# Moving the counts, near_f and the epoch boundaries of a graph layer's planner

## The chip, the cores and the metric

One core of one Trainium2 chip runs the whole program in one launch. The time is the device time of that core in microseconds.

## The reference

For a graph of 6250 nodes and 206250 edges (each random edge in both directions, and a loop at each node) the layer computes a message per edge, a mean over each node's edges, a node network, and a residual layer norm:

```python
msg = jnp.concatenate([x[col], edge_attr], axis=1)       # 64 + 64
h = jax.nn.relu(msg @ W1a.T + b1a) @ W1b.T + b1b         # 128, then 64
sums = segment_sum(h, row, n_nodes)
agg = sums / jnp.maximum(counts, 1.0)[:, None]
z = jax.nn.relu(jnp.concatenate([x, agg], 1) @ W2a.T + b2a) @ W2b.T + b2b
out = jnp.concatenate([z, x], axis=1) @ Wr.T + br
return layernorm(x + out)
```

`row` is the source of an edge, `col` its destination. All is float32. Edges come sorted by destination, so the sources are in no order: the sum over sources is a sort.

## The kernel before

The edges are padded to 1612 tiles of 128 and taken in 124 blocks of 13 tiles (`NG`, `BLK`), in a fixed order that spreads the destinations. The 6250 nodes lie in 49 bins of 128. The fast path sorts edges by bin through memory. A slower general path stands behind it, for inputs that overflow the planner's bounds, which are worked out from means and 4.8 deviations (`SPREAD`).

**A block k** goes through these steps. `group` (three blocks ahead) loads the edge features and the destinations' places; `columns` turns the places into one-hot columns of a window of 64 nodes. `window` computes the first layer's share of those nodes and puts it into the weights `mv`. For the first 8 blocks (`NEAR`) it does this from x itself, and `columns` compares the destinations with `near_f` on VectorE (DVE, L1184). `hidden` (L1206) multiplies 13 tiles of columns by `mv` on TensorE (PE), in portions of 4, 3, 3 and 3 tiles, and ScalarE (ACT, L1209) writes the ReLU into one of five row buffers `orows`. A first write into a buffer (L1507) waits until the scatters of block k-5 have landed.

`carried` and `bins_of` (both two blocks ahead of their use) make one-hots of the edges' bins and scan them along the free axis on DVE (`had`, L936). `counts_of` (L972 to L975, for block k+1) turns them into ranks by PE in a PSUM tile named `cnt`. `slots` reduces those on DVE to an edge's row in memory (`rowidx`, L1000); `quads` does it for joined edges (reading `cnt` up to `at_q`, L1059). `scatter` (called for block k-2) issues one indirect DMA per tile from GpSimd (POOL, L1245). Here the manual order of PE, ACT, DVE, and SyncE (SP) doesn't hold: the framework's scheduler places the scatters, and each block's last ones are held until PE has reached stated points of block k+2.

**Joined groups.** Blocks from `JOIN_FROM` to `JOIN_TO` join the first three tiles (six, in blocks 8 to 61) before they are scattered: `join` (L1115) puts edges of the same bin into rows of four by PE, and one scatter (L1217) writes a joined group into `quads`.

**Sums.** The blocks are parted into four epochs (`EPOCHS`), each with a buffer in memory of its own. A bin has a fixed number of row tiles in each (`cap`), which is what its edges can at most fill; up to `low` tiles are surely filled. When an epoch's scatters, or a stretch of the first epoch's, are done, SP reads its tiles back from four blocks later on (`LATE`), DVE makes one-hots of the nodes (`oh`, L1333), and PE sums (L1352, two PE instructions for a tile). The groups of a stretch are spread evenly over the blocks until the next stretch ends; `groups_at` holds this. `clear` writes zeros ahead of time into the tiles between `low` and `cap`.

**The end.** `nodes_ahead` (L1474 to L1484) computes what the node network needs of x alone, four bins a block from block `PRE`. After the last block the groups of the last epoch are read, summed, and each group is finished and written (`Nodes`).

The iteration for block k (from L1500) has this order on each engine; the start, ahead of it, is: `window(0)`, `carried(0)`, `counts_of(0)`, `columns(0)`, `slots(0)`.

Of the kernel before, what the change touches and what calls it, by code (L numbers as in the profile page):

```python
# [8 lines left out]
F32 = mybir.dt.float32  # L9
# [8 lines left out]
P = 128  # L18
# [430 lines left out]
NG = 13  # L449
WIN = 64  # L450
STEP = 43
EPOCHS = (104, 12, 4, 4)
NEAR = 8
Y_AHEAD = 32
HEAD = 117
# [4 lines left out]
RD = 6  # L460
SUMS, TILES = 3, 12
SEG = 9
PRE = 102
RING = 8
ROWS, EDGES, READS = 5, 4, 9
SPREAD = 4.8
# [1 line left out]
CLEAR = 12  # L468
LEAD = 2
JOIN, QUAD, QROWS = 3, 4, 3  # L470
JOIN_FROM, JOIN_TO = 5, 104
TWICE_FROM, TWICE_TO, TWICE_ROWS = 8, 62, 5
FULLQ = (7, 9)

# [1 line left out]
def order_of(ngr):  # L476


    return [i * STEP % ngr for i in range(ngr)]
# [3 lines left out]
def fast_path(  # L483
# [41 lines left out]
    REM = N - (NB - 1) * P  # L525
    NE = len(EPOCHS)
    W = H + 2
# [4 lines left out]
    order = order_of(NGR)  # L532
    assert NT % NG == 0 and NGR == sum(EPOCHS) and HEAD % BLK == 0 and sorted(order) == list(range(NGR))

# [10 lines left out]
    def joined(k):  # L545
        if not JOIN_FROM <= k < JOIN_TO:
            return 0
        return 2 if TWICE_FROM <= k < TWICE_TO else 1

    def direct(k):  # L550
        return BLK - JOIN * joined(k)
# [39 lines left out]
    epochs, at_blk = [], 0  # L591
    for e, n in enumerate(EPOCHS):
        ep_ = Epoch()
# [25 lines left out]
    qep.first, qep.end = JOIN_FROM, JOIN_TO  # L619
    assert JOIN_TO == EPOCHS[0]  # L620

# [28 lines left out]
    const = ctx.enter_context(tc.tile_pool(name="fconst", bufs=1))  # L650
# [91 lines left out]
    with (  # L742
# [80 lines left out]
        def starts_at(joints):  # L823


            if joints:
                d = BLK - JOIN * joints
                nc.vector.memset(words, 1.0 + 0x3F80 * 2.0**-23)
                v = words.rearrange("p (b t) -> p b t", t=TJ)
                for c in (0, d + 1, TJ, TJ + d + 1):  # L830
                    if c % 2 == 0:
                        nc.vector.memset(v[:, :, c // 2], 1.0)
                    else:
                        nc.vector.memset(v.bitcast(I32)[:, :, c // 2], 0x3F80)
            else:
                v = words[:, : HALF * T]
                nc.vector.memset(v, 1.0 + 0x3F80 * 2.0**-23)
                nc.vector.memset(v.rearrange("p (b t) -> p b t", t=T // 2)[:, :, 0], 1.0)
# [9 lines left out]
        bins(0, HEAD)  # L848

        cnt = slpp.tile([P, 2, 512], F32, name="cnt_ps")  # L850
        near_f = cnt[:, 1, 448 : 448 + NEAR]
        z_ps = steady[:, P + 2 + HALF * TJ :][:, : 2 * JOIN]
        of_first = cnt[:, :, HALF * TJ : HALF * TJ + HALF]
        assert T % 2 == 0 and TJ % 2 == 1
# [60 lines left out]
        def bins_of(k):  # L915


            ep_ = epoch_of[k]
            c0 = k * BLK
            oh = ohs.pop(k)  # L920
            if joined(k) != joined(k - 1):
                starts_at(joined(k))
            t = TJ if joined(k) else T
            had = slp.tile([P, 2 * HALF * t], BF16, name="had", padded_shape=[P, 2 * HALF * TJ])
            by_bin = oh.rearrange("p (b t) -> p b t", t=t)
            d = direct(k)
            for t0, c, n in ((1, c0 + BLK - d, d), (d + 2, c0, BLK - d)):
                if n == 0:
                    continue
                nc.vector.tensor_tensor(  # L930
                    by_bin[:, :, t0 : t0 + n],
                    ramp[:, : 2 * HALF, None].to_broadcast([P, 2 * HALF, n]),
                    hi[:, None, c : c + n].to_broadcast([P, 2 * HALF, n]),
                    op=ALU.is_equal,
                )
            nc.vector.tensor_tensor_scan(had, on[:, : 2 * HALF * t], oh, 0.0, op0=ALU.mult, op1=ALU.add)  # L936
            oh, had = (v.rearrange("p (b t) -> p b t", t=t) for v in (oh, had))
            hads[k] = had
            return oh, had
# [23 lines left out]
        def counts_of(k, oh, had):  # L963
            t = oh.shape[2]

            ps = cnt
            for i in range(2):
                v = ps[:, i, : HALF * t].rearrange("p (b t) -> p b t", t=t)  # L970
                b = slice(i * HALF, (i + 1) * HALF)
                nc.tensor.matmul(v, one_w, had[:, b, :], start=True, stop=False)  # L972
                nc.tensor.matmul(v[:, :, : t - 1], before_w, oh[:, b, 1:], start=False, stop=True)  # L973
                if joined(k) == 2:
                    nc.tensor.matmul(of_first[:, i, :], one_w, had[:, b, direct(k) + 1 + JOIN], start=True, stop=True)  # L975
            return ps
# [171 lines left out]
        def group(g):  # L1148

            rhs = rhss[g % EDGES]  # L1150
            if g < NEAR:
                all_of = dst[g * NG * P : (g + 1) * NG * P].rearrange("(o e) -> o e", o=1)
                s = nc.sync.dma_start(rhs[D:, :].bitcast(I32), all_of.to_broadcast([WIN, NG * P]))
                edges(g)
                with tc.issue_after(s.ins):
                    w = nc.sync.value_load(win_i[0:1, g : g + 1], min_val=0, max_val=N - WIN)
                nc.sync.dma_start(near[:D, g, :], xT[:, bass.ds(w, WIN)])
                return rhs, None, mv[g % MV]
            edges(g)

            half = NG * P // 2
            rel = rhs[D:, :].bitcast(BF16).rearrange("p (h e) -> p h e", h=2)[:, :, half:]
            s = nc.sync.dma_start(
                rel, relt[g : g + 1, :].rearrange("o (h e) -> o h e", h=2).to_broadcast([WIN, 2, half])
            )
            with tc.issue_after(s.ins):
                w = nc.sync.value_load(win_i[0:1, g : g + 1], min_val=0, max_val=N - WIN)
            m = mv[g % MV]
            nc.sync.dma_start(m[D:, :], ytab[bass.ds(w, WIN), :])
            return rhs, rel, m  # L1170

        def columns(g, part_of=0):


            rhs, rel, _ = made[g]
            if g >= NEAR:
                of_win = rhs[D:, :].rearrange("p (h e) -> p h e", h=2)
                if part_of == 0:
                    nc.scalar.activation(of_win, rel, AF.Square, bias=from_win[D:, :])  # L1179
                else:  # L1180
                    nc.scalar.activation(rhs[D:, :], rhs[D:, :], AF.Relu, bias=ones[D:, :1], scale=-1.0)  # L1181
                return
            if part_of == 0:
                nc.vector.tensor_tensor(  # L1184
                    rhs[D:, :], rhs[D:, :].bitcast(I32), near_f[D:, g : g + 1].to_broadcast([WIN, NG * P]),
                    op=ALU.is_equal,
                )

        def window(g):

            ps = hp.tile([P, H], F32, name="h_ps")
            nc.tensor.matmul(ps[D:, :], near[: D + 1, g, :], w1x_t, start=True, stop=True)
            nc.scalar.copy(mv[g % MV][D:, :], ps[D:, :])
# [5 lines left out]
        def hidden(k, parts):  # L1199
            orow = orows[k % ROWS]  # L1200
            rhs, _, m = made[k]
            for k0, n in parts:
                ps = hp.tile([P, SUB, H], F32, name="h_ps")
                for j in range(n):
                    c = k0 + j
                    done[k, c] = nc.tensor.matmul(  # L1206
                        ps[:, j, :], rhs[:, c * P : (c + 1) * P], m, start=True, stop=True
                    ).ins.name
                nc.scalar.activation(orow[:, k0 : k0 + n, :H], ps[:, :n, :], AF.Relu)  # L1209
# [244 lines left out]
        clears.update({6 + 2 * i: (-1, i) for i in range(CLEAR)})  # L1454
        assert max(clears) < EPOCHS[0] and 5 + 2 * CLEAR <= EARLY

# [36 lines left out]
        )  # L1493
        for g in range(3):
            made[g] = group(g)
        window(0)
        carried(0)
        counts = counts_of(0, *bins_of(0))
        columns(0)
        slots(0, counts)  # L1500
        for k, ep_ in enumerate(epoch_of):
# [15 lines left out]
            if k == 0:  # L1517
                hidden(k, ((0, 4), (4, 3), (7, 3), (10, 3)))
                window(1)
                columns(1)  # L1520
                carried(1)
                ahead = bins_of(1)
            if k + 1 < NGR:
                counts = counts_of(k + 1, *ahead)
            if k + 2 < NGR:
                carried(k + 2)
            if k > 0:
                hidden(k, ((0, 4), (4, 3), (7, 3)))
            if k + 2 < NEAR:
                window(k + 2)  # L1530
            if k == NEAR - 6:
# [25 lines left out]
            if k == 4:  # L1557
# [19 lines left out]
                centred(wrx_t)  # L1577
            if 0 <= k - PRE < -(-NB // SUB):
                nodes_ahead((k - PRE) * SUB)
            if k in clears:  # L1580
# [206 lines left out]
```

## Time and profile before

| | |
|---|---|
| three timed runs | 1740.62, 1749.65, 1750.46 us; median 1749.65 |
| profiled execution | 1742.9 us, its span 1741.1 us |
| mean granted clock of TensorE | 0.953 |
| busy: PE, DVE, ACT, POOL | 1495.1 (86%), 1451.1 (83%), 900.1 (52%), 1255.2 us (72%) |
| DMA | 408.89 MB, mean 235 GB/s |
| scatters on POOL | 1153 of single tiles, 153 of joined groups |
| sums on PE (L1352) | 4202 instructions |

A busy share is an average over the stages: the start, blocks 8 to 61 with two joined groups, 62 to 103 with one, the last 20 without, and the end. An engine can set the pace of all of them without being busy all the time, where it has a fixed pause between its instructions. In the timeline, each row is the start, the time, the engine and line, and in brackets the idle time ahead of it with what ended it.

### The profile page before, as it was taken

Reading aid. Unit: us, or ns where it says so; the run is one execution under the profiler, and the core shown is the slowest. Engines: PE = TensorE matmul, PEld = TensorE weight load, DVE = VectorE, ACT = ScalarE, POOL = GpSimd, SP = SyncE. Lnnn points to the kernel's source line nnn. Section 1 sums busy time; section 2 is a strip of 40 time slices with the busy share of each in tenths; the row PEclk is TensorE's granted clock in tenths of the full one; section 3 lists DMA queues with packets and bytes.
Section 4 is the critical chain, followed back from the end, with each engine's and each line's share of the span. In section 5 each row is a group of like instructions: output and inputs, shape, how many; then the busy total and the mean of one; then the engine's idle time right before and its main releaser. Section 6 shows DMA issues by size and latency. Waiting matters only on the chain. (4 is left out here: it accounts for less than half of the span.)

```text
span 1741.1 us, 36105 instructions
## 1 busy us (share of the span) xinstructions
PE 1495.1 (86%) x12229; PEld 1426.3 (82%) x12229; DVE 1451.1 (83%) x3408; ACT 900.1 (52%) x1797; POOL 1255.2 (72%) x1323
## 2 busy tenths in 40 slices
PE   5668888888888888776899999989889999999987
PEld 4568878788878787766798999889889898999976
DVE  8489999999999899766788988989877676888777
ACT  2257777666766666554555555545443333443026
POOL 5777777777777777777777777777777777777720
PEclk9789999989999999978999999999999999999998
DMA  8878888856666565558799999879788888999971
GB/s 185 217 242 273 275 271 271 278 175 190 189 189 189 169 200 169 163 167 238 213 267 271 288 286 276 272 233 269 221 248 255 247 239 252 273 322 298 334 231 47
DMA packets 216190, 408.89 MB, mean 235 GB/s; under 512 B 43265, under 2 KB 122740, under 8 KB 215868
## 3 DMA queue, kind: packets, MB, share of 16 engines
q1 hardware_dynamic: 127770, 230.22, 47.1%
q0 software_dynamic: 49136, 117.56, 20.7%
q10 hardware_dynamic: 39090, 58.69, 10.6%
q8 instruction: 100, 1.64, 0.4%
q14 instruction: 94, 0.77, 0.1%
HBM read 228.29 MB, written 178.01 MB: 233 GB/s over the span
## 5 line engine op out<-in xcount | busy, mean ns | idle before, releaser
L1245 POOL DMA_INDIRECT rows<-orow,rowidx x1153 | 1105.8, 959 | 368.6 <-issue 216.0
L1352 PE MATMUL h_ps<-rt,oh 128*128 128x129 f32 x4202 | 511.4, 280 | 44.8 <-DVE oh L1333 17.4
L1352 PEld LDWEIGHTS h_ps<-rt,oh 128*128 128x128 f32 x4202 | 495.1, 196 | 50.6 <-issue 21.6
L1206 PE MATMUL h_ps<-mv,rhs 128*128 128x128 f32 x3224 | 416.2, 285 | 26.3 <-ACT orow L1209 18.4
L1206 PEld LDWEIGHTS h_ps<-mv,rhs 128*128 128x128 f32 x3224 | 397.5, 200 | 38.8 <-ACT orow L1209 21.3
L1209 ACT ACTIVATE orow<-h_ps 128x512 f32<-128x512 f32 x496 | 255.1, 538 | 302.8 <-PE h_ps L1206 296.2
L1333 DVE TENSOR_TENSOR oh<-ramp,rt 128x512 f32<-128x512 f32 (+4 forms) x466 | 332.3, 752 | 26.9 <-DMA rt<-rows 22.3
L1115 PE MATMUL h_ps<-orow,shared 128*128 128x130 f32 (+1 forms) x2376 | 302.6, 285 | 38.9 <-ACT orow L1209 32.6
L1115 PEld LDWEIGHTS h_ps<-orow,shared 128*128 128x128 f32 x2376 | 291.7, 200 | 43.3 <-ACT orow L1209 37.0
L936 DVE TENSOR_TENSOR_SCAN had<-ramp,bins 128x750 bf16<-128x750 bf16 (+1 forms) x124 | 210.6, 1699 | 99.0 <-ACT bins L956 90.3
L1179 ACT ACTIVATE rhs<-rhs,from_win 64x1664 f32<-64x1664 bf16 x116 | 194.6, 1677 | 2.9
L1181 ACT ACTIVATE rhs<-rhs,ones 64x1664 f32<-64x1664 f32 x116 | 194.6, 1677 | 2.9
L1092 DVE TENSOR_TENSOR shared<-quad_ramp,ramp 128x1536 f32<-128x1536 f32 x99 | 173.4, 1751 | 11.0 <-PE h_ps L1115 4.8
L1507 ACT CAST orow<-lo 128x13 f32<-128x13 bf16 x124 | 26.5, 214 | 292.9 <-DMA rows<-orow,rowidx 256.9
L972 PE MATMUL cnt_ps<-had,one_w 128*128 128x375 bf16 (+1 forms) x248 | 81.8, 332 | 85.5 <-DVE at_q L1059 74.0
L1115 PE MATMUL h_ps<-orow,oh 128*128 128x130 f32 (+1 forms) x1296 | 154.3, 275 | 0.0
L1115 PEld LDWEIGHTS h_ps<-orow,oh 128*128 128x128 f32 x1296 | 149.8, 190 | 0.0
L1119 ACT COPY shared<-h_ps 128x260 f32<-128x260 f32 x168 | 62.2, 378 | 109.2 <-PE h_ps L1115 51.1
L930 DVE TENSOR_TENSOR bins<-ramp,hi 128x300 bf16<-128x300 f32 (+2 forms) x223 | 113.7, 548 | 0.3
L1409 DVE TENSOR_TENSOR part<-part,h_ps 128x387 f32<-128x387 f32 (+2 forms) x207 | 89.9, 435 | 21.2 <-PE h_ps L1352 20.4
L973 PEld LDWEIGHTS <-before_w 128*128 128x128 bf16 x248 | 25.5, 103 | 99.9 <-issue 94.3
L1217 POOL DMA_INDIRECT quads<-shared,qidx x84 | 80.6, 960 | 25.6 <-issue 10.7
(161 smaller groups left out, 1291.9 us busy)
## 6 DMA issues: line engine op xcount, KB each, us to landing
rhs<-in_edgeT SPq DMA_DIRECT2D x124, 416.0 KB
rt<-rows SPq DMA_DIRECT2D x106, 390.0 KB
rt<-rows SPq DMA_DIRECT2D x145, 260.0 KB
rt<-quads SPq DMA_DIRECT2D x97, 260.0 KB
rhs<-relt SPq DMA_DIRECT2D x116, 208.0 KB
rows<-padrow ACTq DMA_DIRECT2D x12, 1560.0 KB
rows<-orow,rowidx POOLq DMA_INDIRECT x1153
rt<-rows SPq DMA_DIRECT2D x48, 325.0 KB
```

Source lines behind the costliest of these rows:

```text
L930: nc.vector.tensor_tensor(by_bin[:, :, t0 : t0 + n], ramp[:, : 2 * HALF, None].to_broadcast([P, 2 * HALF, n]), hi[:, None, c : c + n].to_b ...
L936: nc.vector.tensor_tensor_scan(had, on[:, : 2 * HALF * t], oh, 0.0, op0=ALU.mult, op1=ALU.add)
L1092: nc.vector.tensor_tensor(m, quad_ramp.rearrange("p g q -> p (g q)")[:, None, :].to_broadcast([P, JOIN, QUAD * P]), z_ps[:, i * JOIN : (i ...
L1115: done[k, f"join{i}"] = nc.tensor.matmul(ps[:, j, :w], m[:, t, (g0 + j) * P : (g0 + j + 1) * P], orow[:, i * JOIN + t, :w], start=t == 0, ...
L1179: nc.scalar.activation(of_win, rel, AF.Square, bias=from_win[D:, :])
L1181: nc.scalar.activation(rhs[D:, :], rhs[D:, :], AF.Relu, bias=ones[D:, :1], scale=-1.0)
L1206: done[k, c] = nc.tensor.matmul(ps[:, j, :], rhs[:, c * P : (c + 1) * P], m, start=True, stop=True).ins.name
L1209: nc.scalar.activation(orow[:, k0 : k0 + n, :H], ps[:, :n, :], AF.Relu)
L1245: s = nc.gpsimd.indirect_dma_start(out=ep_.rows, out_offset=bass.IndirectOffsetOnAxis(ap=rowidx[:, k % RING * BLK + j : k % RING * BLK + j ...
L1333: nc.vector.tensor_tensor(res[:, at_tile : at_tile + nb * n, :], ramp[:, None, :].to_broadcast([P, nb * n, P]), node[:, :, None].to_broadc ...
L1352: m = nc.tensor.matmul(of_bin(b), oh[:, at_tile, :], rt[:, j * n + t, : H + 1], start=t0 + t == st.lo[b], stop=t0 + t == st.hi[b] - 1,)
L1409: nc.vector.tensor_add(to, to, g.ps[:, : g.nb, :])
```

## The change

Four things are changed:

- The epochs are 106, 10, 4 and 4 blocks long instead of 104, 12, 4 and 4, and blocks 104 and 105 get a joined group (155 groups instead of 153). `nodes_ahead` starts two blocks later (`PRE`).
- Ahead of the first block, `window(0)` stands behind `counts_of(0)` instead of before `carried(0)`.
- In each block but the first, the first portion of `hidden` (four tiles) stands ahead of `counts_of(k + 1)` and `carried(k + 2)`; the second and third stay behind them.
- `near_f` has an SBUF tile of its own. Before, it lay in a corner of the PSUM tile `cnt`.

```diff
-EPOCHS = (104, 12, 4, 4)
+EPOCHS = (106, 10, 4, 4)
...
-PRE = 102
+PRE = 104
...
-JOIN_FROM, JOIN_TO = 5, 104
+JOIN_FROM, JOIN_TO = 5, 106
...
-        near_f = cnt[:, 1, 448 : 448 + NEAR]
+        near_f = const.tile([P, NEAR], F32, name="near_f")
...
-        window(0)
         carried(0)
         counts = counts_of(0, *bins_of(0))
+        window(0)
         columns(0)
...
+            if k > 0:
+                hidden(k, ((0, 4),))
             if k + 1 < NGR:
                 counts = counts_of(k + 1, *ahead)
             if k + 2 < NGR:
                 carried(k + 2)
             if k > 0:
-                hidden(k, ((0, 4), (4, 3), (7, 3)))
+                hidden(k, ((4, 3), (7, 3)))
```

By the planner's bounds the second epoch's bins then have 4 tiles instead of 5 (the last bin 3 instead of 4), the first epoch's `low` is 16 instead of 15, and the joined rows' last bin has 12 instead of 11.

## The prediction

> **What bounds the kernel now.** First the page: its span, and the costliest group. The two POOL rows are the scatters of single tiles and part of the scatters of joined groups.
>
> ```profile
> span 1741.1 us, 36105 instructions
> ...
> L1245 POOL DMA_INDIRECT rows<-orow,rowidx x1153 | 1105.8, 959 | 368.6 <-issue 216.0
> ...
> L1217 POOL DMA_INDIRECT quads<-shared,qidx x84 | 80.6, 960 | 25.6 <-issue 10.7
> ```
>
> Most of POOL's idle time ends in "issue", so it waits for nothing that the profile shows. The view by stretches (columns: length, then busy us and count of PE, PEld, DVE, ACT, POOL, then clock, DMA share, GB/s) asks whether that holds everywhere.
>
> ```profile
> 120.00:180.00 60.00, 51.38 (x445) 48.81 (x445) 56.74 (x150) 44.38 (x88) 45.26 (x48) 1.00 0.89 274
> ...
> 1440.00:1500.00 60.00, 54.92 (x436) 52.43 (x435) 39.63 (x64) 21.29 (x30) 45.43 (x48) 0.94 0.86 254
> 1500.00:1560.00 60.00, 60.00 (x533) 59.16 (x533) 52.31 (x79) 26.22 (x36) 45.59 (x48) 1.00 1.01 313
> ...
> 1620.00:1680.00 60.00, 53.79 (x463) 53.14 (x462) 45.25 (x103) 0.82 (x2) 38.86 (x41) 0.95 0.86 285
> ```
>
> DVE is nearly full early and PE late, but POOL issues its 48 scatters per 60 us in both. The timeline at POOL's end shows the step:
>
> ```profile
> 1665.05 0.96 POOL L1245 DMA_INDIRECT rows<-orow,rowidx  x1 [0.30 <-DMA rows<-orow,rowidx]
> ...
> 1668.82 2.62 PE L1352 MATMUL h_ps<-rt,oh 128*128 128x129 f32 x22
> ...
> 1670.10 0.96 POOL L1245 DMA_INDIRECT rows<-orow,rowidx  x1 [0.30 <-issue]
> ...
> 1675.92 0.96 DVE L1333 TENSOR_TENSOR oh<-ramp,rt 128x768 f32<-128x768 f32 x1 [4.13 <-DMA rt<-rows]
> ...
> 1676.98 1.41 PE L1352 MATMUL h_ps<-rt,oh 128*128 128x129 f32 x5 [5.54 <-DVE oh L1333]
> ```
>
> Four steps take 5.05 us, so one takes 1.2625 whatever is named behind it. From its first scatter at 17.10 us (row further down) to 1671.06 POOL needs 1654 us; 13 scatters per block less two per joined group make 1306, times 1.2625 gives 1649, and some 5 us are stalls. So POOL is the bound, from its start to its end. Behind it comes a fixed tail of 70 us: the last epoch can be read only when POOL's last scatter has landed. PE had worked off its backlog at 1671.44 and was idle for 5.54 us, so it is a close second.
>
> **The change, part by part.**
>
> *Fewer scatters.* Blocks 104 and 105 now join three tiles each. A joined group replaces three scatters by one: 1302 remain. Four steps less: **-5.05 us**.
>
> *The start.* These rows set POOL's first scatter:
>
> ```profile
> 6.47 1.62 DVE L936 TENSOR_TENSOR_SCAN had<-ramp,bins 128x700 bf16<-128x700 bf16 x1
> ...
> 9.59 0.66 PE L1192 MATMUL h_ps<-w1x_t,rt 65*64 65x128 f32 x2 [9.59 <-DMA rt<-in_xT]
> ...
> 10.28 0.26 ACT L1193 COPY mv<-h_ps 64x128 f32<-64x128 f32 x1 [5.91 <-PE h_ps L1192]
> ...
> 11.03 0.50 PE L973 MATMUL cnt_ps<-bins,before_w 128*128 128x325 bf16 x1
> 11.56 1.89 DVE L1184 TENSOR_TENSOR rhs<-rhs,cnt_ps 64x1664 f32<-64x1664 int32 x1 [3.47 <-PE cnt_ps L973]
> ...
> 13.55 5.37 PE L1206 MATMUL h_ps<-mv,rhs 128*128 128x128 f32 x26 [2.03 <-issue]
> ...
> 15.63 0.60 ACT L1209 ACTIVATE orow<-h_ps 128x512 f32<-128x512 f32 x1 [4.85 <-PE h_ps L1206]
> ...
> 17.10 1.13 POOL L1245 DMA_INDIRECT rows<-orow,rowidx  x1 [13.95 <-DVE rhs L1184]
> ```
>
> DVE's comparison L1184 waits for the counts, only because near_f lies in the counts' own PSUM tile. With near_f in SBUF it can follow the scan at 8.09 and end at 9.98. Counts of block 0 run before the window product, which waits for its own load until 9.59 anyway, so they fill an idle PE. The window's columns are copied by 10.54; that, no longer 13.45, releases L1206. The scatter follows by the same distance: **-2.9 us**. Bounds: the whole 2.9, or none if a later early wait eats it. For block 5, after the loads and table writes of the start, the rows are:
>
> ```profile
> 91.49 1.50 ACT L1209 ACTIVATE orow<-h_ps 128x512 f32<-128x512 f32 x3
> ...
> 97.24 0.96 POOL L1245 DMA_INDIRECT rows<-orow,rowidx  x1 [0.30 <-DMA rows<-orow,rowidx]
> ```
>
> The rows lie ready some 4 us before POOL takes them, more than 2.9. I take the whole.
>
> *near_f in SBUF* also makes L1184 an operation with two SBUF inputs, eight times 1.89 us, seven of them after POOL has started. The nearest rows:
>
> ```profile
> 76.52 0.21 DVE L1048 TENSOR_TENSOR cumq<-n_i,cumq 128x50 f32<-128x50 int32 x1
> ...
> 76.94 0.96 POOL L1245 DMA_INDIRECT rows<-orow,rowidx  x1 [0.30 <-issue]
> ...
> 77.58 1.14 DVE L789 TENSOR_SCALAR rt<-rt,at_f 124x1664 bf16<-124x1664 int32 x1
> ...
> 78.20 1.35 POOL L1245 DMA_INDIRECT rows<-orow,rowidx  x1 [0.31 <-issue]
> ```
>
> Beside L789 a POOL issue took 1.35 instead of 0.96 us; around L1048, with two SBUF inputs but only 0.21 us long, it kept 0.96. I take 0, by L1048; the other end is POOL held for all of seven L1184, 13.2 us. The Trainium skill (SBUF — State Buffer, "SBUF: two separate sides") speaks against this edit: it holds that a VectorE operation with two SBUF inputs takes the port that it shares with GpSimd exclusively against a GpSimd operation that reads SBUF. The pair around L789 agrees that something blocks, the pair around L1048 shows no block; by the rule the sum would be up to 13.2 us higher.
>
> *Counts behind the first four tiles of hidden.* The longest wait that this touches:
>
> ```profile
> PE cnt_ps L972 <- DVE at_q L1059: 74.0, 42, 8.8
> ```
>
> PE fills a part of these waits with four tiles. ACT's first activation moves ahead of its copy of the carried counts, and DVE's scan waits for that copy; but the four tiles last about 1 us and POOL is 4 to 25 us behind the rows there. Both signs are covered by POOL's lag: 0. Without that cover it would cost or bring at most 1 us for a block.
>
> *The sums.* By the planner's own numbers the second epoch needs 4 tiles per bin instead of 5 (3 instead of 4 in the last), 195 instead of 244; the joined rows need one more. So 48 tiles fewer, two PE instructions each, at 0.112 us (84 in 9.38, below): -10.7 us of PE. Two joins add 2 x 2.70. PE's work falls by 5.3 us, but its place moves: the first epoch's last reads and the joined groups' last reads, 42 groups, run over blocks 110-119 instead of 108-119, 98 instructions a block instead of 82, and nodes_ahead runs at 104-116, into that crowd. The chain that ended last gives PE's time for a block, from one hidden (L1206) to the next:
>
> ```profile
> 1209.82 2.70 PE h_ps L1115 x24
> ...
> 1404.14 2.25 PE h_ps L1206 x20
> ...
> 1419.52 2.25 PE h_ps L1206 x20
> ...
> 1438.16 2.25 PE h_ps L1206 x20
> 1446.24 9.38 PE h_ps L1352 x84
> ...
> 1492.94 2.25 PE h_ps L1206 x20
> ...
> 1507.49 2.23 PE h_ps L1206 x20
> ...
> 1559.04 2.23 PE h_ps L1206 x20
> ```
>
> With nodes_ahead (1404.14 to 1492.94, five blocks): 17.8 us, of them 9.1 for 82 sums on average: 8.65 for the rest. Without (1507.49 to 1559.04, four blocks): 12.9, less 9.4 for 84: 3.5. POOL needs 16.4 for a block without a join and 13.9 with one. How far POOL lags behind the rows, at blocks 96 and 114:
>
> ```profile
> 1194.74 1.50 ACT L1209 ACTIVATE orow<-h_ps 128x512 f32<-128x512 f32 x3
> ...
> 1218.00 0.96 POOL L1245 DMA_INDIRECT rows<-orow,rowidx  x1 [0.31 <-issue]
> ...
> 1493.87 1.16 ACT L1209 ACTIVATE orow<-h_ps 128x512 f32<-128x512 f32 x2 [8.44 <-PE h_ps L1206]
> ...
> 1497.07 0.96 POOL L1245 DMA_INDIRECT rows<-orow,rowidx  x1 [0.30 <-issue]
> ```
>
> About 22 us of cover, held there by the five row buffers, had shrunk to 2.6 (the first of the two activations ends at 1494.5). In the changed kernel I start from 22 at block 104. In the built order the first scatters of blocks 104 to 107 follow each other by 12, 12 and 14 places, later ones by 13. Blocks 104 and 105 cost PE 18.0 each (8.65, a join 2.7, sums 6.7) against 15.15: -5.7. Blocks 106-111 cost 16.1 against 17.7 once and 16.4 five times: +3. Blocks 112-115 have 120, 96, 96 and 96 sums, 22.0 and three times 19.4, and 116, with one last bin of nodes_ahead (its like, 1492.94 to 1507.49, had 14.55 with 72 sums), 19.9: 100.1 against 82.1, -18. About 1 us is left at block 117, and afterwards blocks of 14 us win it back. So POOL is at the edge of being starved once, and PE's end (about 1667) stays just ahead of POOL's reading (1669). Bounds: 0, and 10 us if PE's blocks are 0.8 us longer than their mean. I take **+2**, as the estimate lies at the edge. DMA is full at 313 GB/s in 1500-1560 and POOL did not stall there, so the crowded reads add nothing more.
>
> Sum: -5.05 - 2.9 + 2 = -6. The profiled execution took 1742.9 us, so 1736.9. The three timed runs lie on average 4.0 us above it (their median, 1749.65, lies 6.8 above); I add 4: **1741 us**.
>
> **The rivals.**
> - *PE becomes the bound in blocks 104-116.* For: the cover falls to 2.6 already now, and single blocks are worse than the mean (1419.52 to 1438.16: 18.64 with only 72 sums, 10.6 for the rest). Were that the rule, 13 blocks would cost 25 us more, POOL would stand still for some 24, and the result is -7.95 + 24 = +16: 1759, 1763 with the offset. It ends slower from a rest of 9.3 us a block on. Against: the five-block mean is 8.65.
> - *The start's gain is lost* to a later early wait. -5.05 + 2: 1740, 1744 with the offset. For: DMA is busy 0.89 of 120-180 and loads set the early blocks. Against: the cover of block 5.
> - *L1184 holds POOL* by two SBUF inputs: -6 + 13.2 = +7: 1750, 1754 with the offset. The page cited gives it a mechanism; L1048 speaks against.
> - *PE's wait for the counts was the bound after all*: moving them brings up to the 74 us. Against: POOL's unbroken step; so the counts' edit does not do for the time what it does for PE.
>
> **How the numbers follow.** Forecast 0.58, PE-bound 0.14, start lost 0.12, port 0.10, counts 0.02, something not seen 0.04. Range: from both gains whole at the lowest run's offset (1742.9 - 7.95 - 2.3 = 1732.7) to no gain at the start, 10 us of starvation and the highest run's offset (1742.9 - 5.05 + 10 + 7.6 = 1755.4); opened a little: 1731 to 1757. One per cent, about what a measurement of this kernel can tell from no change, is 17.5 us. Faster by that needs the counts' rival or a low run: 0.09. Slower by that: most of the PE-bound case: 0.11. Within: 0.80.
>
> **What would show it.** First scatter at about 14.2 us; 1302 scatters at 1.26; POOL's last ending near 1663 to 1666; 4106 L1352 instructions; PE's wait at L972 shorter with no effect; a POOL stall, if any, near blocks 115-118, its releaser a PE or ACT instruction; a tail of 70 us. Wrong if POOL shows issues much over 0.96 us in the first 100 us, several long waits after 1450 us, or if PE's backlog ends well after POOL.

## The result, and the profile after

In the first comparison the changed kernel took 1751.86 us (median of 21 runs, 1744.82 to 1757.68) and the kernel before 1748.0 us (21 runs): 1.0022 times, 95% interval 1.0012 to 1.0032. Forecast was a gain of 6 us. Two later comparisons, on chips where the kernel before took some 1742 us, gave 0.9991 [0.9982, 1.0000] and 0.9986 [0.9977, 0.9995]; one more, on a chip where PE is slow, is told apart below. So where the kernel before takes 1742 to 1748 us the change is worth no more than a few us either way, and the gain of 6 us came in none of the three. The profiled execution of the changed kernel took 1744.82 us.

The page of the changed kernel, the span and three groups:

```profile
span 1743.0 us, 36099 instructions
...
L1245 POOL DMA_INDIRECT rows<-orow,rowidx x1147 | 1109.1, 967 | 362.6 <-issue 215.1
...
L1352 PE MATMUL h_ps<-rt,oh 128*128 128x129 f32 x4106 | 505.6, 281 | 53.7 <-DVE oh L1333 15.0
...
L1217 POOL DMA_INDIRECT quads<-shared,qidx x86 | 82.8, 962 | 26.9 <-issue 10.7
```

The counts are those forecast (1302 scatters in all, 4106 sums), but six scatters of single tiles fewer take 3.3 us more in all: their mean is 967 ns, not 959. The timeline of the start (start, time, engine and line):

```profile
6.52 1.61 DVE L936 TENSOR_TENSOR_SCAN had<-ramp,bins 128x700 bf16<-128x700 bf16 x1
8.16 1.89 DVE L1184 TENSOR_TENSOR rhs<-rhs,near_f 64x1664 f32<-64x1664 int32 x1
...
9.01 0.50 PE L973 MATMUL cnt_ps<-bins,before_w 128*128 128x325 bf16 x1
...
10.48 4.72 PE L1206 MATMUL h_ps<-mv,rhs 128*128 128x128 f32 x26 [0.35 <-ACT mv L1193]
...
14.06 1.13 POOL L1245 DMA_INDIRECT rows<-orow,rowidx  x1 [11.01 <-ACT orow L1209]
```

This is as forecast: the comparison follows the scan, the first product of `hidden` (L1206) starts at 10.48 instead of 13.55, and POOL starts at 14.06 instead of 17.10. But from 14.06 to the end of its last scatter at 1671.81 POOL now needs 1657.8 us for 1302 scatters. Before, it needed 1654.0 for 1306. Where most of this went is seen in DVE's and POOL's rows set beside each other, from the same timeline:

```profile
16.33 1.89 DVE L1184 TENSOR_TENSOR rhs<-rhs,near_f 64x1664 f32<-64x1664 int32 x1
16.76 2.29 POOL L1245 DMA_INDIRECT rows<-orow,rowidx  x1 [0.30 <-issue]
...
23.13 1.95 DVE L1184 TENSOR_TENSOR rhs<-rhs,near_f 64x1664 f32<-64x1664 int32 x1
23.16 0.96 POOL L1245 DMA_INDIRECT rows<-orow,rowidx  x1 [0.30 <-issue]
24.42 1.49 POOL L1245 DMA_INDIRECT rows<-orow,rowidx  x1 [0.30 <-issue]
...
28.75 0.96 POOL L1245 DMA_INDIRECT rows<-orow,rowidx  x1 [0.30 <-issue]
28.84 1.89 DVE L1184 TENSOR_TENSOR rhs<-rhs,near_f 64x1664 f32<-64x1664 int32 x1
30.02 1.55 POOL L1245 DMA_INDIRECT rows<-orow,rowidx  x1 [0.30 <-issue]
...
34.20 1.89 DVE L1184 TENSOR_TENSOR rhs<-rhs,near_f 64x1664 f32<-64x1664 int32 x1
34.41 2.52 POOL L1245 DMA_INDIRECT rows<-orow,rowidx  x1 [0.30 <-DMA rows<-orow,rowidx]
...
63.38 1.89 DVE L1184 TENSOR_TENSOR rhs<-rhs,near_f 64x1664 f32<-64x1664 int32 x1 [22.43 <-DMA rhs<-in_dst_o]
64.29 1.82 POOL L1245 DMA_INDIRECT rows<-orow,rowidx  x1 [0.31 <-issue]
...
80.77 1.92 DVE L1184 TENSOR_TENSOR rhs<-rhs,near_f 64x1664 f32<-64x1664 int32 x1
82.03 1.50 POOL L1245 DMA_INDIRECT rows<-orow,rowidx  x1 [0.31 <-issue]
```

Six comparisons run after POOL has started (the prediction counted seven, but the one at 11.29 ends ahead of it), and each lengthens one scatter. Add up the ends: the comparison that began at 16.33 ended at 18.22 and the scatter beside it at 19.05; 25.08 and 25.91; 30.73 and 31.57; 36.09 and 36.93; 65.27 and 66.11; 82.69 and 83.53. A scatter that begins while the comparison runs ends 0.83 to 0.84 us after it, however long it has been going. One that begins with it, as at 23.16, gets through in 0.96. A scatter begins every 1.26 us and a comparison lasts 1.89, so each comparison catches one. Over 0.96 us these six lost 1.33 + 0.53 + 0.59 + 1.56 + 0.86 + 0.54 = 5.4 us.

The crowded blocks, from the same timeline: the first activation and POOL's first scatter of block 117.

```profile
1543.16 0.60 ACT L1209 ACTIVATE orow<-h_ps 128x512 f32<-128x512 f32 x1 [10.53 <-PE h_ps L1206]
...
1546.86 0.96 POOL L1245 DMA_INDIRECT rows<-orow,rowidx  x1 [0.30 <-issue]
```

The rows were ready at 1543.76, so 3.1 us of cover were left, less than in any block from 108 on; in this execution POOL was not starved. In four of the seven other profiles with the new stretches on chips where POOL sets the pace (those with added comparisons left out), it stood still at just this block and waited for these rows: 1.0 and 1.4 us in the later profiles of the changed kernel, 1.3 with the scalar compare, and longest with the stretches alone (both experiments follow):

```profile
1540.86 0.95 POOL L1245 DMA_INDIRECT rows<-orow,rowidx  x1 [2.69 <-ACT orow L1209]
```

The end, and PE's wait at the counts in the view of waits (us in all, times, longest):

```profile
1670.85 0.96 POOL L1245 DMA_INDIRECT rows<-orow,rowidx  x1 [0.30 <-issue]
...
1672.33 6.05 PE L1352 MATMUL h_ps<-rt,oh 128*128 128x129 f32 x52 [0.22 <-PE h_ps L1352]
...
1679.29 2.06 DVE L1333 TENSOR_TENSOR oh<-ramp,rt 128x768 f32<-128x768 f32 x2 [0.56 <-DMA rt<-rows]
...
1680.35 2.92 PE L1352 MATMUL h_ps<-rt,oh 128*128 128x129 f32 x24 [1.97 <-DVE oh L1333]
```

```profile
PE cnt_ps L972 <- DVE at_q L1059: 54.3, 33, 7.9
```

PE's backlog now ends at 1678.4, 6.6 us behind POOL's last scatter (0.4 before). The last epoch's first sums begin at 1680.35, 8.5 us behind that scatter. In the kernel before it was 5.9 us, and in all five profiles where PE waited 3.4 us or longer at this place 5.9 to 6.3. So here PE, with the reads that wait for it, came later than POOL's rows would have let it. The tail from POOL's end to the span's end is 71.2 us (70.1 before). PE's wait at the counts fell by 20 us (74.0 before), and no time came of it.

### The profile page after: what moved, and what is told of

It is laid out like the page before. It is cut to its first block, busy times and chain, and to the rows that moved or that the text cites. A ratio compares the mean times of both kernels' runs of the same rounds, so it can differ in the third digit from the quotient of the medians.

```text
span 1743.0 us, 36099 instructions
## 1 busy us (share of the span) xinstructions
PE 1502.5 (86%) x12181; PEld 1431.5 (82%) x12181; DVE 1450.0 (83%) x3428; ACT 891.6 (51%) x1805; POOL 1260.6 (72%) x1319
## 4 chain that ended last, share of the span: by engine, by line
PE 38%; DMA 21%; DVE 21%; issue 7%; ACT 6%; POOL 5%; ACTq 1%; SPq 0%; DVEq 0%; POOLq 0%
PE h_ps L1352 19%; DMA rows<-orow,rowidx 16%; PE h_ps L1206 8%; PE h_ps L1115 6%; DVE had L936 4%; POOL rows L1245 4%; DMA quads<-shared,qidx 3%; DVE shared L1092 3%; DVE oh L1092 2%; ACT rhs L1179 2%; DVE row L993 1%; DVE bins L930 1%; ACT orow L1209 1%; PE h_ps L801 1%; DMA quads<-rt,qidx 1%
## 5 line engine op out<-in xcount | busy, mean ns | idle before, releaser
L1352 PE MATMUL h_ps<-rt,oh 128*128 128x129 f32 x4106 | 505.6, 281 | 53.7 <-DVE oh L1333 15.0
L1352 PEld LDWEIGHTS h_ps<-rt,oh 128*128 128x128 f32 x4106 | 487.9, 197 | 60.4 <-issue 19.3
L1206 PE MATMUL h_ps<-mv,rhs 128*128 128x128 f32 x3224 | 431.4, 283 | 19.6 <-ACT of_q L1121 13.0
L1206 PEld LDWEIGHTS h_ps<-mv,rhs 128*128 128x128 f32 x3224 | 403.1, 198 | 31.3 <-ACT of_q L1121 13.6
L1209 ACT ACTIVATE orow<-h_ps 128x512 f32<-128x512 f32 x496 | 261.8, 542 | 271.2 <-PE h_ps L1206 266.7
L1115 PE MATMUL h_ps<-orow,shared 128*128 128x130 f32 (+1 forms) x2424 | 313.2, 288 | 57.4 <-ACT orow L1209 51.0
L1115 PEld LDWEIGHTS h_ps<-orow,shared 128*128 128x128 f32 x2424 | 299.9, 201 | 64.6 <-ACT orow L1209 57.8
L1333 DVE TENSOR_TENSOR oh<-ramp,rt 128x512 f32<-128x512 f32 (+3 forms) x466 | 324.5, 737 | 31.2 <-DMA rt<-rows 25.9
L972 PE MATMUL cnt_ps<-had,one_w 128*128 128x375 bf16 (+1 forms) x248 | 81.7, 331 | 70.5 <-DVE at_q L1059 54.3
L1092 DVE TENSOR_TENSOR oh<-quad_ramp,ramp 128x1536 f32<-128x1536 f32 x54 | 94.3, 1747 | 0.0
```

The costliest lines, as they stand in the source:

```text
L1092: nc.vector.tensor_tensor(m, quad_ramp.rearrange("p g q -> p (g q)")[:, None, :].to_broadcast([P, JOIN, QUAD * P]), z_ps[:, i * JOIN : (i ...
L1115: done[k, f"join{i}"] = nc.tensor.matmul(ps[:, j, :w], m[:, t, (g0 + j) * P : (g0 + j + 1) * P], orow[:, i * JOIN + t, :w], start=t == 0, ...
L1206: done[k, c] = nc.tensor.matmul(ps[:, j, :], rhs[:, c * P : (c + 1) * P], m, start=True, stop=True).ins.name
L1333: nc.vector.tensor_tensor(res[:, at_tile : at_tile + nb * n, :], ramp[:, None, :].to_broadcast([P, nb * n, P]), node[:, :, None].to_broadc ...
L1352: m = nc.tensor.matmul(of_bin(b), oh[:, at_tile, :], rt[:, j * n + t, : H + 1], start=t0 + t == st.lo[b], stop=t0 + t == st.hi[b] - 1,)
```

## The experiments

The theory: the comparison L1184, which now reads two SBUF operands, holds POOL's issue, and this eats what the start and the stretches bring. Its rivals: the crowded sums, the moved counts, or the new place of near_f as such.

### One part at a time

The stretches alone, on the kernel before:

```diff
-EPOCHS = (104, 12, 4, 4)
+EPOCHS = (106, 10, 4, 4)
-PRE = 102
+PRE = 104
-JOIN_FROM, JOIN_TO = 5, 104
+JOIN_FROM, JOIN_TO = 5, 106
```

> The kernel before with the epochs alone (106, 10, 4, 4, joined groups to block 105, nodes_ahead from 104); counts and near_f as before. Theory A (near_f's place costs POOL time at the start, the epochs are sound): four steps of 1.2625 us less, some 2.5 us of it lost at the end where the sums now finish later: 2.5 to 5 us faster than before, no POOL issue much over 0.96 us beside L1184, first scatter at 17.1. Theory B (the crowded last sums cost the time): 3 us or more slower than before, with POOL stalls near block 117 or sums that end 5 us or more behind POOL.

Measured: 1738.17 us, 0.9977 [0.9967, 0.9988] of the kernel before (1742.5, measured beside it). -4.3 us; POOL ends at 1665.5 instead of 1671.05.

Everything but the stretches:

```diff
-        near_f = cnt[:, 1, 448 : 448 + NEAR]
+        near_f = const.tile([P, NEAR], F32, name="near_f")
...
-        window(0)
         carried(0)
         counts = counts_of(0, *bins_of(0))
+        window(0)
...
+            if k > 0:
+                hidden(k, ((0, 4),))
...
-                hidden(k, ((0, 4), (4, 3), (7, 3)))
+                hidden(k, ((4, 3), (7, 3)))
```

> The change without the epochs: counts moved, window(0) moved and near_f in SBUF, but 104, 12, 4, 4 and 153 joined groups. Theory A: first scatter at 14.1 us (3.0 earlier), then six or seven POOL issues of 1.5 to 2.5 us beside L1184, 5.4 us in all: 2.4 us slower than before. Theory B: only the 3 us of the start are left: 3 us faster than before.

Measured: 1746.14 us, 1.0020 [1.0011, 1.0030]. POOL starts at 14.08 and ends at 1673.1, 2 us later than before, with 1306 scatters in both. 3 us are won at the start and 5 lost after it.

Of that, the place of near_f alone (the first of the three edits):

> The kernel before with near_f's SBUF tile alone; order and epochs as before. L1184 need not wait for the counts, so the first scatter comes at about 15 us (2 earlier, since the counts still stand behind the window on PE). Theory A: the issues beside the seven later L1184 grow by 5.4 us in all: 3 us slower than before. Theory B: 2 us faster than before.

Measured: 1745.54 us, 1.0022 [1.0009, 1.0036]. POOL starts at 14.70, so this edit alone frees 2.4 us of the start, and POOL ends at 1672.4. After its start POOL needs 3.7 us more than before for the same 1306 scatters. This edit is the loss.

### near_f back in PSUM, where it waits for nothing

The changed kernel whole, but the comparison reads a PSUM column of its own, outside the counts' tile:

```diff
+        near_at = steady[:, P + 2 + HALF * TJ + 2 * JOIN :][:, :1]
...
+                nc.vector.tensor_copy(near_at[D:, :], near_f[D:, g : g + 1])
                 nc.vector.tensor_tensor(
-                    ..., near_f[D:, g : g + 1].to_broadcast([WIN, NG * P]),
+                    ..., near_at[D:, :].to_broadcast([WIN, NG * P]),
```

> The changed kernel, but ahead of each L1184 VectorE copies its column of near_f into the one spare column of the PSUM tile that holds ramp, and L1184 reads it there: one SBUF and one PSUM input, no tie to the counts. Theory A: POOL issues beside L1184 back at 0.96 us, first scatter still at about 14.2: 5.4 us faster than the changed kernel, 1 to 2 us faster than before or equal to it. Theory B: as the changed kernel, 4 us slower than before.

Measured: 1735.68 us, 0.9959 [0.9946, 0.9971]. POOL's group on this kernel's page, and the timeline around the first comparison behind POOL's start:

```profile
L1247 POOL DMA_INDIRECT rows<-orow,rowidx x1147 | 1100.7, 960 | 364.9 <-issue 212.9
```

```profile
16.77 0.96 POOL L1247 DMA_INDIRECT rows<-orow,rowidx  x1 [0.30 <-issue]
...
17.08 1.89 DVE L1186 TENSOR_TENSOR rhs<-rhs,ramp 64x1664 f32<-64x1664 int32 x1
...
18.04 0.96 POOL L1247 DMA_INDIRECT rows<-orow,rowidx  x1 [0.31 <-issue]
```

The same comparison, as long, and a scatter that begins inside it takes 0.96 (the trace names the PSUM tile with the new column `ramp`). The start keeps its 3 us (POOL at 14.08), and the gain is close to the 6 us of the forecast: -6.8 us.

### The dose

To that kernel 36 more comparisons of the same size are added, one in each of blocks 64 to 99, once with near_f in SBUF and once with the PSUM column as the second operand. They write a tile that is filled again later; nothing reads them.

```diff
+            if 64 <= k < 100:
+                nc.vector.tensor_tensor(
+                    xr[D:, :26, :], ones[D:, None, :D].to_broadcast([WIN, 26, D]),
+                    near_f[D:, :1].to_broadcast(...), op=ALU.is_equal,     # or near_at[D:, :]
+                )
```

> e_near_column with one more VectorE comparison in each of the blocks 64 to 99 (36 of them, 64 x 1664, result not used by anything), whose second input is near_f in SBUF. VectorE has room there. Theory A: POOL issues that meet one grow by some 0.9 us on average, as the 5.4 us over six issues of the changed kernel do: 25 to 35 us slower than e_near_column, all of it in blocks 64 to 99. Rival (the early issues grew for another reason, such as full DMA queues at the start): 0.

> The same 36 comparisons with the second input in the spare PSUM column. Theory A: 0 against e_near_column. Rival (VectorE's added time itself costs): as e_dose_sbuf.

Measured: 1767.9 us with SBUF (1.0160 [1.0142, 1.0179]), 1751.19 with PSUM (1.0046 [1.0032, 1.0060]). With SBUF, one of the added comparisons and the scatter behind it in the timeline, and POOL's groups:

```profile
1011.78 1.89 DVE L1594 TENSOR_TENSOR xr<-ones,near_f 64x1664 f32<-64x1664 f32 x1
1012.20 2.30 POOL L1247 DMA_INDIRECT rows<-orow,rowidx  x1 [0.30 <-issue]
```

```profile
L1247 POOL DMA_INDIRECT rows<-orow,rowidx x1147 | 1127.4, 983 | 361.4 <-issue 219.5
...
L1219 POOL DMA_INDIRECT quads<-shared,qidx x86 | 88.4, 1028 | 27.0 <-issue 10.7
```

Against the kernel with the column, the single scatters' busy time rose by 1127.4 - 1100.7 = 26.7 us and that of this group of joined ones by 5.9 (82.5 there): 32.6 us for 36 comparisons, 0.9 each, and 32 us in the time. The pair above ends at 1013.67 and 1014.50, again 0.83 apart, and so does every one of the 36 pairs (0.83 to 0.84).

With PSUM the group's mean stays 959 ns, so the added work as such lengthens no scatter:

```profile
L1247 POOL DMA_INDIRECT rows<-orow,rowidx x1147 | 1100.5, 959 | 379.7 <-issue 210.4
```

But it was not free, as its expectation had it. DVE was full where the comparisons stood (first row, the view by stretches), and later POOL waited for rows (second row, the timeline):

```profile
1100.00:1300.00 200.00, 177.46 (x1475) 172.17 (x1474) 192.25 (x411) 103.09 (x175) 149.99 (x157) 0.97 0.85 250
```

```profile
1534.63 0.96 POOL L1247 DMA_INDIRECT rows<-orow,rowidx  x1 [3.60 <-ACT orow L1211]
```

Such waits come at 1477, 1495, 1515, 1535 and 1555, once a block: 2 to 4 us each. This is the first rival of the prediction, brought about from outside: with the cover gone, the crowded blocks starve POOL. In the kernel with SBUF POOL was itself so late that this could not show.

### The moved counts

The kernel with the column, but the counts ahead of hidden in each block, as before:

```diff
-            if k > 0:
-                hidden(k, ((0, 4),))
...
-                hidden(k, ((4, 3), (7, 3)))
+                hidden(k, ((0, 4), (4, 3), (7, 3)))
```

> near_f's column in PSUM and the epochs of the changed kernel, but the counts of each block ahead of the first four tiles of hidden as before; window(0) stays behind counts of block 0. Theory A: the move of the counts in each block is worth nothing, since POOL never waits for it: as e_near_column, 0.4% faster than before, first scatter at 14.1 us; PE's wait at L972 back to some 74 us from what e_near_column has. Rival: the move brings a part of the gain, and this run is 0.2% or more behind e_near_column.

> The changed kernel once more, since its profile had a POOL step of 1.266 us from start to end where before had 1.263, worth 3.9 us over 1302 scatters. Theory A1 (the step is a matter of the execution, the edits simply add up): the order alone was 0.20% slower, the epochs alone 0.23% faster, so 0.03% faster or equal; step 1.263 in the profile, POOL issues beside L1184 longer by 5 to 7 us in all. Theory A2 (the step belongs to this program): 0.2% slower again and step 1.266 again.

Measured: 1733.22 us, 0.9958 [0.9944, 0.9972], against 0.9959 with the counts moved. So in each block the move is worth nothing that these two intervals, some 2 us either way, can show. The changed kernel, unaltered and measured beside it, gave 1740.08, 0.9991 [0.9982, 1.0000], 6.9 us above the other, from which it differs in the column and in the counts.

### Another bound: a chip on which PE is slow

The next four ran on a chip where the kernel before took 2370 us.

> The kernel before itself, for its profile beside the changed kernel's on one chip. Ratio 1.000. If the POOL step is a matter of chip or execution, it is the same here as in the changed kernel's profile of this call; if it belonged to the program, 1.263 here and 1.266 there.

> The changed kernel a third time: so far 0.22% slower in one comparison and 0.09% faster in another, each with an interval of 0.1%. From the parts measured alone (order +0.20%, epochs -0.23%) within 0.1% of before; if the first comparison was the rule, 0.2% slower.

> The changed kernel with L1184 as a tensor_scalar whose second operand is near_f's column in SBUF as one scalar per partition: one SBUF stream in, one out. If a second SBUF stream alone holds POOL: issues stay at 0.96, 0.4% faster than before like e_near_column. If such an operation runs in the faster mode that L789 and L728 to L730 seem to have (1664 columns in about 1 us), it is half as long but holds POOL as they do, by 0.4 to 0.7 us in each of some six issues: 3 us behind e_near_column.

> e_column_old_counts once more beside the others of this call, as the version that may beat both kernels: 0.4% faster than before, POOL's only longer issues those beside L789 and L728 to L730.

Measured, as ratios to the kernel before: itself 0.9998 [0.9969, 1.0027]; the changed kernel 0.9832 [0.9796, 0.9868]; the one with a scalar compare 0.9843 [0.9808, 0.9878]; the column with the counts as before 0.9921 [0.9895, 0.9946]. The page of the kernel before says what is different (TensorE's mean granted clock was 0.828, against 0.953):

```profile
span 2384.6 us, 36105 instructions
...
L1245 POOL DMA_INDIRECT rows<-orow,rowidx x1153 | 1105.6, 959 | 932.1 <-ACT orow L1209 324.4
L1352 PE MATMUL h_ps<-rt,oh 128*128 128x129 f32 x4202 | 691.3, 317 | 263.2 <-issue 242.5
```

POOL's scatters take what they took, but POOL waits 932 us instead of 369 ahead of them, over half of the surplus for rows that ACT copies late. So POOL is not the bound, and its holds cost nothing that shows. What PE does counts, and there the kernels with the moved counts stand ahead. One wait of PE in the kernel before, the changed kernel and the last one, a fence each (us in all, times, longest):

```profile
PE h_ps L1115 <- ACT orow L1209: 68.3, 23, 10.3
```

```profile
PE h_ps L1115 <- ACT orow L1209: 10.9, 9, 4.4
```

```profile
PE h_ps L1116 <- ACT orow L1211: 71.5, 29, 4.7
```

It falls from about 70 to 11 us with the counts behind the first four tiles (to 16 in the kernel with the scalar compare). The two kernels with the counts moved are the two faster ones, by 0.8% or some 19 us. That this wait makes the 19 us is not shown: the last kernel differs from the changed one in the column too, and in the profiles of the first comparison, where POOL is the bound, the same wait rose with the change, from 32.6 to 51.0 us. Why this chip ran slower than its clock alone would make it stays open (PE's 242 us in "issue" were 14 in the profile before).

### All on one chip

On one more chip the changed kernel, the scalar compare and the column (with the counts as before) were measured together. The scalar compare takes near_f from SBUF, one value per partition, in 1.09 us:

```diff
-                nc.vector.tensor_tensor(
-                    ..., near_f[D:, g : g + 1].to_broadcast([WIN, NG * P]), op=ALU.is_equal,
+                nc.vector.tensor_scalar(..., near_f[D:, g : g + 1], None, op0=ALU.is_equal)
```

> The changed kernel as it is, against the kernel before, a third time on whatever chip comes. Open is why the same two kernels gave +0.22% on one chip, -0.09% on a second and -1.7% on a third whose clock was 0.83 to 0.85. If POOL bounds (clock near 0.95, POOL's gaps after its start a few us in all) the sum of the measured parts is -3.0 (start) - 4.3 (stretches) + 6.5 (holds beside L1184) = -0.8 us, so a ratio of 0.998 to 1.002, with the sign set by how many of the seven L1184 happen to fall on a long issue: 5 to 8 us of early excess. If the throttle is down on this chip too and POOL idles hundreds of us, the ratio follows PE: 0.98 to 0.99.

> The changed kernel with L1184 as a compare with one scalar per partition instead of a broadcast tensor: near_f stays in SBUF, the operation takes 1.09 us in place of 1.89. Where PE bounded, its trace already showed POOL's issues lengthened by 0.24 to 0.86 us beside four of these, 2.9 us early excess in all against 6.3 for the changed kernel. If the hold is what cost the changed kernel its gain, then where POOL bounds this one stands 3 to 4 us below it: 0.996 to 0.999 of the kernel before. If the place of near_f as such (its way to SBUF, its later arrival) is what costs, it stands where the changed kernel stands.

> Column in PSUM, new stretches, window(0) ahead, counts ahead of the hidden products as in the kernel before. Where POOL bounds: 0.995 to 0.997 of the kernel before, as on the second chip (0.9958), early excess under 2 us. Set beside the changed kernel in the same call it gives the price of the holds without a change of chip: 6 to 8 us. Where PE bounds (throttle down) it should be 0.985 to 0.995.

Measured: 1739.7 us (0.9986 [0.9977, 0.9995]), 1739.3 (0.9982 [0.9973, 0.9991]), 1735.92 (0.9962 [0.9949, 0.9975]). The kernel with the column stands 3.8 us below the changed one, less than the 6 to 8 expected. The scalar compare was to stand 3 to 4 us below the changed kernel and stood 0.4 below. Its own holds are shorter but there, and of two kinds, as its timeline has it:

```profile
21.50 1.09 DVE L1184 TENSOR_SCALAR rhs<-rhs,near_f 64x1664 f32<-64x1664 int32 x1
22.05 1.36 POOL L1244 DMA_INDIRECT rows<-orow,rowidx  x1 [0.30 <-ACT orow L1208]
...
61.32 1.52 POOL L1244 DMA_INDIRECT rows<-orow,rowidx  x1 [0.30 <-issue]
61.63 1.09 DVE L1184 TENSOR_SCALAR rhs<-rhs,near_f 64x1664 f32<-64x1664 int32 x1 [22.61 <-DMA rhs<-in_dst_o]
...
1676.49 2.92 PE L1351 MATMUL h_ps<-rt,oh 128*128 128x129 f32 x24 [1.32 <-issue]
```

The first pair ends at 22.59 and 23.41: the same 0.82 us, with one tensor operand. So two SBUF tensors are not the only condition; this form holds POOL too. The second pair is another kind: the scatter was already 0.31 us under way when the comparison began, and it ended 0.12 us after it (62.72 and 62.84). Four of the six held scatters end so, three of which began ahead of the comparison. The tensor form did not do that: beside it, scatters that had begun 0.09 and 0.36 us earlier kept 0.96 (first profile).

A reason why the scalar form is not better in the time shows in the profiled executions, one of each kernel. Its six holds add 2.3 us, those of the changed kernel on this chip 5.8, as expected, and POOL needs only 1.0 us more than with the column (1650.6 and 1649.6). But its tail is 74.2 us against 70.5: PE's backlog ends 10.4 us behind POOL's last scatter (0.9 with the column), and PE goes on to the last epoch (the last row above, 1.32 us in "issue") without a wait for its reads. So, in this execution, what the shorter holds won in POOL was lost to PE at the end. Against the changed kernel's profile POOL needs 6.0 us less, of which 3.9 are the longer plain scatters of that execution (told further down), and the tail is 1.4 us longer: that leaves 0.7 us, near the 0.4 measured. Whether PE is late there by the moved counts or by its granted clock is open: between 1300 and 1420 us and between 1420 and 1540 us the clock was 0.91 and 0.94, and 0.96 and 0.97 in the kernel with the column.

## Why the prediction was wrong, and where it was right

**The step that failed** is the price of near_f in SBUF, taken as 0 from L1048; it was 5.4 us in the profile. That row could not bear it. It ran from 76.52 to 76.73, and the scatter quoted beside it began at 76.94: the two never overlapped as the comparisons and scatters do here. In the same profile 24 scatters do begin while an L1048 runs, and all took 0.96. But if a scatter ends 0.83 us after such an operation, one of 0.21 us can't lengthen it by more than 0.08 (0.21 + 0.83 - 0.96), so no L1048 could have shown a hold. The other pair of the prediction had the law in it. L789 ended at 77.58 + 1.14 = 78.72 and the scatter at 78.20 + 1.35 = 79.55, 0.83 us later, as in every pair of a comparison in tensor form since. Read so, a comparison of 1.89 us that meets a scatter every 1.26 costs between 0.5 us (the scatter begins late in it) and 1.7 (it begins early), one scatter each time: for six, 3 to 10 us. Measured: 5.4, and 0.9 for each of the 36 added. The bound of 13.2 us was right as a bound, the rival that held it had the mechanism, and the chance given to it (0.10) was too low.

The Trainium skill (SBUF — State Buffer, "SBUF: two separate sides") states the mechanism, and the prediction weighed it and set it aside for L1048. The trace agrees on the VectorE side: the scatter is held until the comparison ends. It differs on the other side. By the page the GpSimd operation too would keep the ports for its whole instruction; here a comparison that began 0.09 us after a scatter (28.75 and 28.84) took its usual 1.89 us, and the longest delay seen in this kernel was 0.06 (1.95 at 23.13). And of the scalar compare's scatters, three that were under way first were held all the same.

**The other steps.** The start: -2.9 forecast, -3.0 in the trace; the kernel with the column against the stretches alone, -2.5 us in the time. Four scatters less: -5.05, and with the crowded blocks +2 a sum of -3; measured -4.3 us for the stretches alone. The crowd: "about 1 us is left at block 117" was 3.1 at just that block in the first profile, and 1.0 to 2.7 us too little in four others; so the step had the block and the releaser right and the size to within some 4 us, and +2 was a fair price, though the first profile did not pay it. The dose with PSUM showed the same place with less cover. The counts in each block: 0 forecast, 0 measured where POOL sets the pace. That PE's backlog ends just ahead of POOL's reading (1667 against 1669) did not hold: it ended at 1678.4, 6.6 us behind POOL, and the last sums began 8.5 us behind POOL instead of 5.9, so 2.6 us later. The prediction had this among its signs of being wrong. It cost little in the first profile, as the tail is only 1.1 us longer than before, and more in the one with the scalar compare.

**The sum again**, with the failed term mended: -3.0 - 4.3 + 5.4 = -1.9 us. The second and third comparisons have -2.3 and -2.4. The first has +3.9, and that 6 us are not explained. A part of it can be named. In the profiled execution of that comparison all scatters were a little longer. The changed kernel's profile beside the scalar compare shows it again (first row), that of the same kernel under "The moved counts" does not (second row):

```profile
L1245 POOL DMA_INDIRECT rows<-orow,rowidx x1147 | 1109.4, 967 | 361.7 <-issue 211.1
```

```profile
L1245 POOL DMA_INDIRECT rows<-orow,rowidx x1147 | 1106.7, 965 | 362.9 <-issue 206.9
```

Both means hold the lengthened scatters too; the median scatter takes 962 ns in the first execution and 958 in the second. From one scatter to the next it is 1.266 us against 1.263, which makes 3.9 us over 1302. With it the first two profiled executions add up. POOL's stream should be -5.05 + 5.4 + 3.9 = 4.2 us longer and is 3.8; with -3.0 at the start and +1.1 in the tail that makes the +1.9 us between them (1742.9 and 1744.82). The 3 ns are not in the program alone, as the same program ran without them. The first row's execution was the longest of its twelve (1745.21, median 1739.7), so that they come and go with the execution is likely, not shown. Whether the 21 timed runs of the first comparison had them can't be seen: only profiled executions leave a trace, and that one was the shortest of its 21.

The forecast for the runs also leaned on an offset of 4 us from three runs (5.1 in the 21 runs of the kernel before); it was as uncertain as the effect. That 1751.86 lies inside the stated 1731 to 1757 is luck: the range was opened for a starved POOL and for the spread of the runs, not for the holds.

## What to carry to other kernels

Where GpSimd issues scatters one after the other and sets the pace, a VectorE operation beside it can have a second price that its own engine doesn't show: here the tensor form with both operands in SBUF and the scalar form had it, and the tensor form with an operand in PSUM had not. Look in the timeline at the issues that overlap it, and see when they end. An operation as short as 0.21 us can't show it. An operand that stands in PSUM to no purpose may be what keeps two engines apart; if it is in the way there, give it another PSUM column before moving it to SBUF (here 0.996 of the time instead of 0.999 to 1.002). And find out which engine sets the pace on the chip at hand: the kernels with the counts moved gained nothing by it that showed with POOL as the bound, and stood 0.8% ahead where PE was.

## What the runs showed of the hardware

- A comparison of 64x1664 on VectorE with its second operand in SBUF holds a GpSimd scatter that begins during it: the scatter ends 0.83 us after the comparison, against 0.96 us alone. With the operand in PSUM the scatter keeps 0.96. So 0.13 us of the scatter seem to pass beside the comparison. A scatter that began up to 0.8 us ahead of the comparison kept 0.96.
- A comparison of 64x1664 in scalar form (1.09 us, one value per partition from SBUF) also holds a scatter that was already 0.09 to 0.31 us under way when it began: that scatter ends 0.12 us after it. Those that began 0.56 and 0.71 us ahead kept 0.96.
- The plain scatter took 958 to 959 ns in most profiled executions and 962 in two of the changed kernel's.
- On one chip the kernel before took 2370 us instead of 1742, with a granted clock of 0.83: PE's waits in "issue" grew (242 us ahead of L1352, 14 before), and POOL, which waited 932 us ahead of its scatters, was no longer the bound.
